# Attention's four units together ahead of the graph convolution, with one denominator fold, in batches 2 to 14

## The chip, the cores and the metric

The kernel runs on one core of one Trainium2 chip. The core has a matrix engine (TensorE, in the profile PE, with its weight loads as PEld), a vector engine (VectorE, DVE), a scalar engine (ScalarE, ACT), a small general engine (GpSimd, POOL) and a synchronisation engine whose queue issues the transfers (SyncE, SP). They run side by side, each strictly in the order of its own instructions, and wait for each other through semaphores. TensorE writes only to PSUM; the other compute engines read it there.

The metric is the device time of one execution in microseconds (us). The kernel before took 2126.58 us, the median of three runs (2126.36 to 2126.92). Lower is better.

## The reference

Sixteen graphs ("batches") of 1024 nodes with 256 channels go through two layers. Cut to what matters:

```python
# layer 0: attention whose queries come from a data-dependent weighting of the adjacency
c_adj = mean(x, channels)                            # one number a node
A  = abs(abs(sigmoid(c_adj[None] - c_adj[:, None]) - .5) - .5) * 2
g  = relu((x.T @ (adj * (A + A.T) / 2)) * para)      # queries, 4 heads of 64
k, v = split(x @ kv_w)
x  = layernorm(x + softmax(q @ k.T * scale) @ v)
# layer 1: two graph convolutions
h  = relu(x @ w1_loop + adj @ (x @ w1_neigh) + b1)
h  = relu(h @ w2_loop + adj @ (h @ w2_neigh) + b2)
x  = layernorm(x + (x + h) * .5)
```

Everything is float32 and everything stays on one core.

## The kernel before, in words

**Stages of a batch.** In the steady state (batches 2 to 14) the kernel works on four batches at once. In the turn of batch b TensorE does, in this order:

1. scores and outputs of attention units 0 and 1 of batch b (a unit is one pair of heads, `pair`, and one half of the 1024 query nodes, `j`; four units in `UNITS`);
2. one joined convolution (`Joined.run`) that does the first convolution of batch b-1 (`c1`) and the second of batch b-2 (`c2`) together, as seven products in the manner of Strassen: products 1, 2, 6, 7, 5, 4, 3 in this order, then seven smaller products with the second layer's weights (`last_products`);
3. scores and outputs of units 2 and 3 of batch b;
4. the queries of batch b+1 (`FastQueries`, seven products for each of four steps, tiles `g_ps`);
5. keys and values of batch b+1 (`KeysValues`).

The scores (`scores`, L702 in the profile before) make 8 tiles of 128 x 1024 a unit in PSUM; ScalarE takes their exponential into rows `pr`; the outputs (`outputs`, L744) multiply them with the values. The softmax denominators are sums of the `pr` rows: VectorE adds the eight rows of a unit (`collect`, L721 and L723), transposes the sum in 32 x 32 blocks and reduces it (`partial`, L728 and L731), and a small product with a constant `fold` on TensorE (`add`, L764) finishes them. `add` then scales the outputs, adds the residual and reduces (L770 to L777). `turn` (L755) takes an output out of PSUM by a block transpose.

**Memories.** Nearly all working data lie in 31 rows of 128 x 1024 in SBUF (tag `row`), given out in turn: a new tile waits for the last readers and writers of the tile that had its place. PSUM is given out in the same way: three tiles of two banks (`big_psum`, `half_psum` takes half of one) and two tiles of one bank (`bank_psum`). Of each four score tiles one is split in two halves over the two single banks (`split` in `scores`: tiles 2 and 6 of unit 0 and 2, and so on); an output takes a half of a big tile (first unit of a pair) or a single bank (second unit).

**What sets the order.** The order on every engine is the order in which the program is written (`manual_schedule`). Nothing is moved by a scheduler; the kernel places VectorE's and ScalarE's work for the queries, the layer norms and the convolution by hand, as functions that run between two products (`between`, called by `turn_to`). SyncE's one queue issues all transfers in program order, and its wait for a row holds back every later transfer. The adjacency is read from memory in each batch, 512 KB a row: seven pairs of rows for the convolution (`Joined.fetch`, L198) and eight rows for the queries (`Queries.load`, L544).

In the turn of batch b the other engines have, beside the above: the likenesses of the queries (`likeness`, two ScalarE passes over 128 x 1024 each, L560 and L561), their product with the adjacency (`times_adj`, L566) and sums (`right`, L619 to L622) on VectorE; sums over 128 x 512 blocks on GpSimd (`Joined.left`, tiles `R`, and `FastQueries.left`, tiles `S`); sums for keys and values on VectorE (`KeysValues.sums`, L423 to L431); two layer norms (`BlockedNorm`; `statistics`, `deviation`, `finish_aside`).

Of the kernel before, what the change touches and what calls it, by code (L numbers as in the profile page):

```python
# [18 lines left out]
def kernel(  # L19
# [310 lines left out]
    def by_node(t):  # L330
        return t.rearrange("p (bn r) -> p bn r", r=S)
# [252 lines left out]
    class FastQueries(Queries):  # L584
# [16 lines left out]
        def block(self, i, j):  # L601
            return self.xb[:, j * TJ:(j + 1) * TJ, ts(i, P)]

        def left(self, eng):
            s12, s34 = (row_tile(f"S_{self.b}_{k}").rearrange("p (s t c) -> p s t c", s=2, c=P) for k in range(2))
            eng.tensor_add(s12[:, 0], self.block(1, 0), self.block(1, 1))
            eng.tensor_sub(s12[:, 1], s12[:, 0], self.block(0, 0))
            eng.tensor_sub(s34[:, 0], self.block(0, 0), self.block(1, 0))
            eng.tensor_sub(s34[:, 1], self.block(0, 1), s12[:, 1])
            self.S = [s12[:, 0], s12[:, 1], s34[:, 0], s34[:, 1]]  # L610
# [63 lines left out]
    class Attention:  # L674
# [5 lines left out]

        def __init__(self, b, xB, qT, kT, v):
            self.b, self.xB, self.qT, self.kT, self.v = b, xB, qT, kT, v
            self.parts, self.o, self.pr = {}, {}, {}

            self.rden = small.tile([P, len(UNITS) * FB // S], F32, tag="rden", name=f"rden_{b}", bufs=2)
            self.sums = small.tile([P, NC, NB], F32, tag="sums", name=f"sums_{b}", bufs=2)
# [38 lines left out]
        def partial(self, u):  # L725
            b = self.b
            accB = row_tile(f"accB_{b}_{u}")
            nc.vector.transpose(accB, self.acc)  # L728
            if u % 2 == 0:
                self.part = small.tile([P, 2, N // S], F32, tag="den_part", name=f"den_part_{b}_{u}", bufs=2)  # L730
            nc.vector.tensor_reduce(self.part[:, u % 2, :], by_node(accB), AX.X, ALU.add)  # L731
            self.parts[u] = self.part

        def both_scores(self, pair, summed=True):
            for j in range(NJ):
# [15 lines left out]
        def turn(self, u):  # L751
# [2 lines left out]
            self.o[u] = work.tile([P, FB], F32, tag="o", name=name) if late else row_tile(name)[:, 0:FB]  # L754
            nc.vector.transpose(self.o[u], pav)  # L755

        def add(self, *units):

            b, half = self.b, FB // S
            u0, n = units[0], len(units)  # L760
            pd = bank_psum(f"den_ps_{b}_{u0}")
            den = pd[:, 0:2 * half * n]
            part = [self.parts.pop(u) for u in units][0]
            nc.tensor.matmul(den, fold.rearrange("p a k -> p (a k)"),  # L764
                             part[:, u0 % 2:u0 % 2 + n, :].rearrange("p u k -> p (u k)"), start=True, stop=True)
            den = den.rearrange("p (u s h) -> p u s h", u=n, s=2)
            rden = self.rden[:, u0 * half:(u0 + n) * half].rearrange("p (u h) -> p u h", u=n)
            for s in range(2):
                rows = slice(s * HD, (s + 1) * HD)
                nc.vector.reciprocal(rden[rows], den[rows, :, s, :])  # L770
            for k, u in enumerate(units):
                pair, j = UNITS[u]
                o = by_node(self.o.pop(u))
                nc.vector.tensor_mul(o, o, rden[:, k, :].unsqueeze(2).to_broadcast([P, half, S]))
                dst = by_node(self.xB[pair][:, ts(j, FB)])
                nc.vector.tensor_add(dst, dst, o)
                nc.vector.tensor_reduce(self.sums[:, pair, ts(j, half)], dst, AX.X, ALU.add)  # L777
            if u == len(UNITS) - 1:
                join(self.sums)
# [324 lines left out]
    class Joined:  # L1104
# [33 lines left out]
        def run(self, between=None, last=None):  # L1138
# [17 lines left out]
            self.product(2, third)  # L1156
            nc.vector.tensor_add(p1, p1, third)
            turn_to(2)
            if last:
                bias(third, b2_sb[:, ts(0, P)])  # L1160
                if c2.w2 is None:
                    c2.load_sums()
            self.product(6, first, again=True)
            nc.scalar.copy(u1, first)
            c1.relu(0, p1)
            turn_to(6)
            self.product(7, second, start=True)
            nc.scalar.copy(p7, second)
            turn_to(7)
            self.product(5, first, again=True)  # L1170
            nc.scalar.copy(u3, first)
# [26 lines left out]
    def run():  # L1198
# [58 lines left out]
        for b in range(B):  # L1257
# [18 lines left out]
                q.times_adj(TJ)  # L1276
                q.right(0)

            def two_units(pair, before_first=lambda: None, before_second=lambda: None):
                u = NJ * pair  # L1280
                att.outputs(u, half_psum, turned=False)
                before_first()
                att.turn(u)
                att.outputs(u + 1, turned=False)
                before_second()
                att.turn(u + 1)

            if more and not c1:
                att.both_scores(0)
                NodeSums(q, xb, str(b + 1)).all()  # L1290
                two_units(0)
                att.both_scores(1)
                for t in range(3):
                    q.load(t)
                    q.weigh(t)
                two_units(1)
            elif more and not both:
                att.scores(0)
                att.outputs(0)
                NodeSums(q, xb, str(b + 1)).all()  # L1300
                kv = KeysValues(b + 1, channel_major(blocked, f"xT_{b + 1}"))
                att.scores(1)
                kv.sums()
                att.add(0)
                att.outputs(1)
                for t in (0, TJ):
                    q.load(t)
                c1.inner()
                q.left(nc.gpsimd)
                for t in (0, TJ):  # L1310
                    q.likeness(t)
                for ij, n in QUARTERS.items():
                    store(n, quarters[ij])
                c1.first(quarters, lambda: (att.add(1), adj_sums(quarters, 1), adj_sums(quarters, 2), weigh_first()))
                c1.turn_blocks()
                att.scores(2)
                att.outputs(2)
                for t in (1, TJ + 1):
                    q.load(t)
                    q.likeness(t)  # L1320
                    q.times_adj(t)
                att.scores(3)
                for t in (2, TJ + 2, 3, TJ + 3):
                    q.load(t)
                for t in (2, TJ + 2, 3, TJ + 3):
                    q.likeness(t)
                q.right(1)
                att.add(2)
                att.outputs(3)
            elif more:  # L1330
                att.both_scores(0, summed=False)
                nodes = NodeSums(q, xb, str(b + 1))
                att.collect(1, 1, 2, 3)
                nodes.turn()
                att.collect(1, *range(4, NT))
                att.partial(1)
                both.fetch("00", "10")
                c2.load_x()

                def next_xT():  # L1340
                    ready["xT"] = channel_major(blocked, f"xT_{b + 1}")

                two_units(0, before_second=next_xT)
                if c3:
                    c3.statistics()
                kv = KeysValues(b + 1, ready["xT"])
                kv.sums()
                both.fetch(2, 3)
                nodes.line()
                both.fetch(1)  # L1350
                nodes.row()
                for t in (0, TJ):
                    q.load(t)
                both.fetch(4, "11")
                c1.inner()
                both.left(nc.gpsimd)
                q.left(nc.gpsimd)
                both.run({1: (lambda: q.likeness(0),),
                          2: (lambda: att.add(0, 1), lambda: q.likeness(TJ), lambda: c3 and c3.deviation(), weigh_first)},
                         last=nc.gpsimd)  # L1360
                c1.turn_blocks()
                att.both_scores(1)
                order = (1, TJ + 1, 2, TJ + 2, 3, TJ + 3)
                for t in order:
                    q.load(t)
                for t in order:
                    q.likeness(t)

                def weigh_second():
                    q.times_adj(1)  # L1370
                    q.times_adj(TJ + 1)
                    q.right(1)

                two_units(1, before_second=weigh_second)
            else:
                att.both_scores(0)
                two_units(0)
                att.both_scores(1)
                two_units(1, before_second=lambda: att.add(0, 1))
# [38 lines left out]
            elif more:  # L1418
                q.pair(2)
                q.step(0)  # L1420
                if c3:
                    c3.finish_aside(out[b - 3])
                q.step(1, lambda: att.add(*((2, 3) if both else (3,))), 5)
                q.pair(3)
                q.step(2, norm.mean)
                q.load_para()
                kv.load()
                q.step(3)
# [107 lines left out]
```

## Time and profile before

The profiled execution took 2127.08 us, 0.50 us above the median of the three runs; its span from first to last instruction is 2125.2 us. The granted TensorE clock was 0.999 of full speed. Stages of the turn of batch 8 (start 1045.54 us, length 130.74 us, as in nearly all turns of batches 3 to 14), from the profile's table by stretches of time:

| stage of the turn | us | DVE busy | ACT busy | POOL busy | GB/s |
|---|---|---|---|---|---|
| scores and outputs, units 0 and 1 | 27.82 | 26.27 | 18.18 | 3.49 | 278 |
| joined convolution | 37.85 | 33.59 | 11.72 | 15.41 | 125 |
| scores and outputs, units 2 and 3 | 27.82 | 25.82 | 20.55 | 0.00 | 128 |
| queries of the next batch | 24.59 | 23.99 | 14.02 | 0.00 | 124 |
| keys and values of the next batch | 12.66 | 10.43 | 7.50 | 4.96 | 172 |
| sum | 130.74 | 120.11 | 71.97 | 23.86 | |

TensorE is busy through all of it. How to read this: "busy" is the time in which an engine executes; a table row of a timeline names the start, the length, the engine, the line of the kernel, the tiles and how many equal instructions follow each other, and in brackets the idle time before and what ended it. A float32 product appears as two matrix instructions, and products with 64 rows of two heads run side by side, so 64 instructions of the scores are 16 tiles.

### The profile page before, as it was taken

How to read it: one execution, taken by the hardware profiler on the slowest of the kernel's cores; microseconds unless marked ns; L12 is line 12 of the kernel's file. 1: busy time of each engine (PE TensorE's matmuls, PEld its weight loads, DVE VectorE, ACT ScalarE, POOL GpSimd, SP SyncE). 2: the span in 40 equal slices, each digit the busy share in tenths (PEclk: the TensorE clock that was granted, in tenths of full speed). 3: DMA queues.
4: the chain of work that ended last, by engine and by line, in shares of the span. 5: the costliest groups of instructions: out<-in, count | busy, mean ns of one | idle time of the engine just before them, and what ended most of it. 6: DMA issues, size and time to landing. Idle time of an engine off the chain costs nothing.

```text
span 2125.2 us, 25170 instructions
## 1 busy us (share of the span) xinstructions
PE 2115.0 (100%) x8734; PEld 1036.0 (49%) x8734; DVE 1907.4 (90%) x2381; ACT 1139.7 (54%) x1669; POOL 358.6 (17%) x209
## 2 busy tenths in 40 slices
PE   9999999999999999999999999999999999999998
PEld 5344444545445455454554444544445444454354
DVE  6899998989999899998989989899898998989975
ACT  5745545555365563655636556355564556555523
POOL 2010120121302213031130311303013130121021
PEclk9999999999999999999999999999999999999999
DMA  9495766637539275492845929468293682934555
GB/s 214 121 179 188 135 228 140 177 107 152 210 109 258 95 146 197 129 273 70 166 170 136 264 70 191 152 152 241 70 221 122 159 233 70 253 100 123 152 167 177
DMA packets 613718, 346.39 MB, mean 163 GB/s; under 512 B 491984, under 2 KB 556880, under 8 KB 613584
## 3 DMA queue, kind: packets, MB, share of 16 engines
q1 hardware_dynamic: 613312, 344.45, 62.0%
q8 instruction: 71, 1.16, 0.2%
q14 instruction: 63, 0.52, 0.1%
q10 hardware_dynamic: 272, 0.26, 0.0%
HBM read 294.45 MB, written 50.20 MB: 162 GB/s over the span
## 4 chain that ended last, share of the span: by engine, by line
PE 97%; SPq 1%; DMA 1%; DVE 0%; ACT 0%; issue 0%; POOL 0%; POOLq 0%; DVEq 0%
PE s L702 21%; PE av L744 21%; PE hu_ps L1135 17%; PE g_ps L647 16%; PE v_ps L448 4%; PE k_ps L444 4%; PE hu_ps L972 4%; PE t_ps L858 3%; PE hu_ps L865 2%; PE g_ps L574 1%; PE h_ps L880 1%; PE u_ps L909 1%; PE h_ps L972 1%; SPq L108 1%; SPq L229 0%; DMA adj<-in_adj_dram 0%
## 5 line engine op out<-in xcount | busy, mean ns | idle before, releaser
L723 DVE TENSOR_TENSOR acc<-acc,pr 128x1024 f32<-128x1024 f32 x384 | 472.2, 1230 | 37.4 <-DVE acc L723 1.4
L702 PE MATMUL s<-qT,kT 64*128 64x512 f32 x2048 | 449.7, 593 | 0.2 <-ACT qT L581 0.2
L744 PE MATMUL av<-pr,v 128*64 128x512 f32 x2048 | 447.0, 594 | 0.0
L709 ACT ACTIVATE pr<-s 128x1024 f32<-128x1024 f32 x392 | 391.8, 1122 | 75.3 <-PE s L702 75.2
L702 PEld LDWEIGHTS s<-qT,kT 64*128 64x128 f32 x2048 | 196.3, 187 | 233.0 <-issue 183.0
L744 PEld LDWEIGHTS av<-pr,v 128*64 128x64 f32 x2048 | 144.0, 137 | 297.4 <-issue 272.9
L361 POOL TENSOR_TENSOR rstd<-rstd,neg_half 128x32 f32<-128x32 f32 x16 | 99.2, 6203 | 1112.8 <-DVE rstd L359 1112.8
L1135 PE MATMUL hu_ps<-adj,R 128*128 128x512 f32 x480 | 214.3, 594 | 0.0
L560 ACT ACTIVATE wg<-c_row,c_sums 128x1024 f32<-128x1024 f32 x120 | 137.0, 1142 | 81.4 <-DVE den_part L731 60.3
L566 DVE SCALAR_TENSOR_TENSOR wg<-wg,adj 128x1024 f32<-128x1024 f32 x128 | 150.0, 1210 | 3.6 <-ACT wg L561 3.6
L707 ACT ACTIVATE pr<-s 128x512 f32<-128x512 f32 x240 | 143.3, 710 | 0.3 <-PE s L702 0.3
L1135 PEld LDWEIGHTS hu_ps<-adj,R 128*128 128x128 f32 x480 | 89.0, 190 | 100.9 <-issue 98.8
L561 ACT ACTIVATE wg<-wg 128x1024 f32<-128x1024 f32 x128 | 135.3, 1057 | 4.1
L861 ACT COPY t<-t_ps 128x1024 f32<-128x1024 f32 x16 | 16.2, 1012 | 189.8 <-PE t_ps L858 189.8
L647 PE MATMUL g_ps<-wg,S 128*128 128x512 f32 x224 | 115.6, 597 | 0.0
L647 PE MATMUL g_ps<-T,S 128*128 128x512 f32 x224 | 115.5, 597 | 0.0
L647 PE MATMUL g_ps<-wg,x 128*128 128x512 f32 x224 | 109.0, 599 | 0.0
L1135 PE MATMUL hu_ps<-adj,t 128*128 128x512 f32 x240 | 105.7, 592 | 0.0
L1126 POOL TENSOR_TENSOR R<-h 128x512 f32<-128x512 f32 x14 | 28.2, 2012 | 359.5 <-PE av L744 238.5
L721 DVE TENSOR_TENSOR acc<-pr,pr 128x1024 f32<-128x1024 f32 x64 | 77.5, 1210 | 11.9 <-ACT pr L709 11.9
L728 DVE STREAM_TRANSPOSE accB<-acc 128x1024 f32<-128x1024 f32 x64 | 79.7, 1245 | 2.2
L731 DVE TENSOR_REDUCE den_part<-accB 128x32 f32<-128x1024 f32 x64 | 78.1, 1220 | 2.2
(235 smaller groups left out, 3116.9 us busy)
## 6 DMA issues: line engine op xcount, KB each, us to landing
adj<-adjT SPq DMA_DIRECT2D x210, 512.0 KB
adj<-in_adj_dram SPq DMA_DIRECT2D x128, 512.0 KB
para<-in_L_gnn_para_dram SPq DMA_DIRECT2D x32, 512.0 KB
xB_a<-in_x_dram SPq DMA_DIRECT2D x128, 128.0 KB
x1d<-xB_a SPq DMA_DIRECT2D x128, 128.0 KB
x<-x1d SPq DMA_DIRECT2D x16, 1024.0 KB
xB<-in_x_dram SPq DMA_DIRECT2D x120, 128.0 KB
x<-in_x_dram SPq DMA_DIRECT2D x15, 1024.0 KB
```

Of the source, the lines that this page charges most:

```text
L361: nc.gpsimd.tensor_tensor(self.rstd, self.rstd, neg_half, ALU.pow)
L560: nc.scalar.activation(wg, self.c_row, AF.Abs, bias=self.c_col[:, t:t + 1], scale=-1.0)
L561: nc.scalar.activation(wg, wg, AF.Tanh, scale=-0.5 / C)
L566: nc.vector.scalar_tensor_tensor(wg, wg, 1.0, self.adj.pop(t), op0=ALU.add, op1=ALU.mult)
L647: nc.tensor.matmul(self.p[n], x_n[:, k, :], w_n, start=(k == 0), stop=(k == TJ - 1))
L702: nc.tensor.matmul(halves[s], self.kT[rows, pair, ts(mt, P)], self.qT[rows, pair, ts(j, FB)], start=True, stop=True)
L707: nc.scalar.activation(pr[:, ts(s, FB)], halves[s], AF.Exp)
L709: nc.scalar.activation(pr, ps, AF.Exp)
L723: nc.vector.tensor_add(self.acc, self.acc, prs[mt])
L744: nc.tensor.matmul(pav[s * HD:(s + 1) * HD, :], self.v[:, mt, pair * P + s * HD:pair * P + (s + 1) * HD], prs[mt][:, ts(s, FB)], start=(mt ...
L972: nc.tensor.matmul(dst[:, ts(t, P)], a[:, ts(t, P)], w, start=first, stop=True, skip_group_check=not first)
L1135: nc.tensor.matmul(dst, self.x[n][:, k, :], of_rows(rows, k), start=(start and k == 0), stop=(k == TJ - 1), skip_group_check=again)
```

## The change

In batches 2 to 14 (the branch with both convolutions) the order of the turn becomes: units 0 and 1, units 2 and 3, joined convolution, queries, keys and values. What moves with it:

- `both_units` replaces `both_scores` and `two_units` there. The first unit of a pair adds up its rows as its scores come; of the second unit the additions follow on VectorE, with the block transpose of the first output between the fifth and the sixth addition, and that of the second output after `partial`. Both outputs go into the halves of one row. NodeSums and its transpose (`sums`, `nodes.turn`), the two first query rows' likenesses and the first transfers for the convolution stand between them.
- `add_all` replaces the two calls of `add`: one fold over the denominators of all four units (a 128 x 128 product in place of two of 128 x 64), two reciprocals in place of four, and multiplication, addition and reduction on 1024 columns at a time (six instructions in place of twelve). It stands after product 2 of the convolution. `den_part` becomes one tile for all units.
- The query rows are weighed in another order: 0 and 4 during attention and after product 1, 1 and 5 between products 1 and 4, 2, 6, 3 and 7 after the convolution's last products, with the layer norm's `finish_aside` behind them.
- VectorE's transpose of the next batch's input (`channel_major`) comes after all of attention; GpSimd's query sums `S` go into the rows of that input (`q.left(nc.gpsimd, blocked)`); the layer norm's statistics and deviation follow together; the sums for keys and values move to the last step of the queries.
- In `Joined.run` ScalarE's copy of the bias into the third bank comes after product 7's copy, not after product 2.
- The transfers: convolution rows 00 and 10 and query rows 0 and 4 are fetched during units 2 and 3, then 2 and 3; 1, query rows 1 and 5, 4 and 11 after them. The store of the first layer's output (`turn_blocks`) comes after the whole convolution and now stands right ahead of the queries.

```diff
+        def both_units(self, pair, first=lambda: None, second=lambda: None, third=lambda: None):
+            u = NJ * pair
+            self.scores(u, 0)
+            self.scores(u + 1, NT, summed=False)
+            row = row_tile(f"o_{self.b}_{pair}")
+            self.collect(u + 1, 1)
+            first()
+            self.collect(u + 1, 2, 3)
+            second()
+            self.outputs(u, half_psum, turned=False)
+            self.collect(u + 1, 4, 5)
+            pav, self.o[u] = self.o[u], row
+            nc.vector.transpose(row[:, 0:FB], pav)
+            self.collect(u + 1, 6, 7)
+            self.partial(u + 1)
+            self.outputs(u + 1, turned=False)
+            third()
+            nc.vector.transpose(row[:, FB:N], self.o.pop(u + 1))
+
+        def add_all(self):
+            b, half, n = self.b, FB // S, len(UNITS)
+            pd = bank_psum(f"den_ps_{b}")
+            nc.tensor.matmul(pd[:, 0:n * NB], fold.rearrange("p a k -> p (a k)"),
+                             self.part.rearrange("p u k -> p (u k)"), start=True, stop=True)
...
+            for pair in range(NC):
+                o = by_node(self.o.pop(NJ * pair))
+                nc.vector.tensor_mul(o, o, self.rden[:, ts(pair, NB)].unsqueeze(2).to_broadcast([P, NB, S]))
+                dst = by_node(self.xB[pair])
+                nc.vector.tensor_add(dst, dst, o)
+                nc.vector.tensor_reduce(self.sums[:, pair, :], dst, AX.X, ALU.add)
+            join(self.sums)
...
             turn_to(2)
-            if last:
-                bias(third, b2_sb[:, ts(0, P)])
-                if c2.w2 is None:
-                    c2.load_sums()
+            if last and c2.w2 is None:
+                c2.load_sums()
             self.product(6, first, again=True)
...
             nc.scalar.copy(p7, second)
+            if last:
+                bias(third, b2_sb[:, ts(0, P)])
             turn_to(7)
...
             elif more:
-                att.both_scores(0, summed=False)
-                nodes = NodeSums(q, xb, str(b + 1))
-                att.collect(1, 1, 2, 3)
-                nodes.turn()
-                att.collect(1, *range(4, NT))
-                att.partial(1)
-                both.fetch("00", "10")
-                c2.load_x()
...
-                two_units(0, before_second=next_xT)
...
+                att.both_units(0, sums, lambda: nodes.turn())
+                nodes.line()
+                nodes.row()
+                att.both_units(1, before_convolution, third=lambda: (q.times_adj(0), q.times_adj(TJ)))
+                c1.inner()
+                xT_next = channel_major(blocked, f"xT_{b + 1}")
+                both.left(nc.gpsimd)
+                q.left(nc.gpsimd, blocked)
...
-                both.run({1: (lambda: q.likeness(0),),
-                          2: (lambda: att.add(0, 1), lambda: q.likeness(TJ), lambda: c3 and c3.deviation(), weigh_first)},
+                both.run({1: (lambda: q.likeness(1), lambda: q.likeness(TJ + 1), lambda: q.right(0)),
+                          2: (att.add_all,),
+                          4: (lambda: q.times_adj(1), lambda: q.times_adj(TJ + 1)),
+                          3: (more_weights, lambda: q.right(1))},
                          last=nc.gpsimd)
                 c1.turn_blocks()
-                att.both_scores(1)
...
-                two_units(1, before_second=weigh_second)
...
                 q.pair(2)
                 q.step(0)
-                if c3:
-                    c3.finish_aside(out[b - 3])
-                q.step(1, lambda: att.add(*((2, 3) if both else (3,))), 5)
+                if both:
+                    q.step(1)
+                else:
+                    q.step(1, lambda: att.add(3), 5)
                 q.pair(3)
                 q.step(2, norm.mean)
+                if both:
+                    kv.sums()
```

More of the change, by code (lines that the diff above doesn't have):

```diff
@@ L602, in block, with left @@
             return self.xb[:, j * TJ:(j + 1) * TJ, ts(i, P)]
-        def left(self, eng):
-            s12, s34 = (row_tile(f"S_{self.b}_{k}").rearrange("p (s t c) -> p s t c", s=2, c=P) for k in range(2))
+        def left(self, eng, rows=None):
+            rows = rows or [row_tile(f"S_{self.b}_{k}") for k in range(2)]
+            s12, s34 = (row.rearrange("p (s t c) -> p s t c", s=2, c=P) for row in rows)
             eng.tensor_add(s12[:, 0], self.block(1, 0), self.block(1, 1))
@@ L682, in __init__ @@
             self.b, self.xB, self.qT, self.kT, self.v = b, xB, qT, kT, v
-            self.parts, self.o, self.pr = {}, {}, {}
+            self.o, self.pr = {}, {}
             self.rden = small.tile([P, len(UNITS) * FB // S], F32, tag="rden", name=f"rden_{b}", bufs=2)
@@ L728, in partial @@
             nc.vector.transpose(accB, self.acc)
[L729 to L732, printed above, removed]
+            if u == 0:
+                self.part = small.tile([P, len(UNITS), N // S], F32, tag="den_part", name=f"den_part_{b}", bufs=1)
+            nc.vector.tensor_reduce(self.part[:, u, :], by_node(accB), AX.X, ALU.add)
         def both_scores(self, pair, summed=True):
@@ L755, in turn @@
             nc.vector.transpose(self.o[u], pav)
+        def both_units(self, pair, first=lambda: None, second=lambda: None, third=lambda: None):
[21 more added lines that the diff above has]
+                             self.part.rearrange("p u k -> p (u k)"), start=True, stop=True)
+            den = pd[:, 0:n * NB].rearrange("p (u s h) -> p u s h", u=n, s=2)
+            rden = self.rden.rearrange("p (u h) -> p u h", u=n)
+            for s in range(2):
+                rows = slice(s * HD, (s + 1) * HD)
+                nc.vector.reciprocal(rden[rows], den[rows, :, s, :])
+            for pair in range(NC):
[5 more added lines that the diff above has]
+            join(self.sums)
         def add(self, *units):
@@ L762, in add @@
             den = pd[:, 0:2 * half * n]
-            part = [self.parts.pop(u) for u in units][0]
             nc.tensor.matmul(den, fold.rearrange("p a k -> p (a k)"),
-                             part[:, u0 % 2:u0 % 2 + n, :].rearrange("p u k -> p (u k)"), start=True, stop=True)
+                             self.part[:, u0:u0 + n, :].rearrange("p u k -> p (u k)"), start=True, stop=True)
             den = den.rearrange("p (u s h) -> p u s h", u=n, s=2)
@@ L1277, in weigh_first, with two_units @@
                 q.right(0)
-            def two_units(pair, before_first=lambda: None, before_second=lambda: None):
+            def two_units(pair, before_second=lambda: None):
                 u = NJ * pair
                 att.outputs(u, half_psum, turned=False)
-                before_first()
                 att.turn(u)
@@ L1330, in run @@
             elif more:
-                att.both_scores(0, summed=False)
-                nodes = NodeSums(q, xb, str(b + 1))
-                att.collect(1, 1, 2, 3)
-                nodes.turn()
-                att.collect(1, *range(4, NT))
-                att.partial(1)
-                both.fetch("00", "10")
-                c2.load_x()
-                def next_xT():
-                    ready["xT"] = channel_major(blocked, f"xT_{b + 1}")
-                two_units(0, before_second=next_xT)
@@ L1344, in run, with sums, before_convolution @@
-                if c3:
[L1345 to L1349, printed above, removed]
+                nodes = None
+                def sums():
+                    nonlocal nodes
+                    nodes = NodeSums(q, xb, str(b + 1))
+                    c2.load_x()
+                def before_convolution():
+                    both.fetch("00", "10")
+                    for t in (0, TJ):
+                        q.load(t)
+                        q.likeness(t)
+                    both.fetch(2, 3)
@@ new lines, in run @@
+                att.both_units(0, sums, lambda: nodes.turn())
[6 more added lines that the diff above has]
+                q.left(nc.gpsimd, blocked)
+                if c3:
+                    c3.moments()
+                kv = KeysValues(b + 1, xT_next)
@@ L1350, in run, with more_weights @@
                 both.fetch(1)
-                nodes.row()
-                for t in (0, TJ):
+                for t in (1, TJ + 1):
                     q.load(t)
                 both.fetch(4, "11")
-                c1.inner()
-                both.left(nc.gpsimd)
-                q.left(nc.gpsimd)
-                both.run({1: (lambda: q.likeness(0),),
-                          2: (lambda: att.add(0, 1), lambda: q.likeness(TJ), lambda: c3 and c3.deviation(), weigh_first)},
+                def more_weights():
+                    for t in (2, TJ + 2, 3, TJ + 3):
+                        q.load(t)
+                        q.likeness(t)
+                    if c3:
+                        c3.finish_aside(out[b - 3])
@@ L1360, in run @@
+                both.run({1: (lambda: q.likeness(1), lambda: q.likeness(TJ + 1), lambda: q.right(0)),
+                          2: (att.add_all,),
+                          4: (lambda: q.times_adj(1), lambda: q.times_adj(TJ + 1)),
+                          3: (more_weights, lambda: q.right(1))},
                          last=nc.gpsimd)
                 c1.turn_blocks()
-                att.both_scores(1)
-                order = (1, TJ + 1, 2, TJ + 2, 3, TJ + 3)
-                for t in order:
-                    q.load(t)
@@ L1366, in run @@
[L1366 to L1372, printed above, removed]
-                two_units(1, before_second=weigh_second)
             else:
```

## The prediction

> **What bounds the kernel now.** I read the page first: engine shares, then the chain that ended last.
>
> ```profile
> span 2125.2 us, 25170 instructions
> PE 2115.0 (100%) x8734; PEld 1036.0 (49%) x8734; DVE 1907.4 (90%) x2381; ACT 1139.7 (54%) x1669; POOL 358.6 (17%) x209
> PE 97%; SPq 1%; DMA 1%; DVE 0%; ACT 0%; issue 0%; POOL 0%; POOLq 0%; DVEq 0%
> ```
>
> The chain is TensorE almost alone, so only two things can change the time: TensorE's own instructions, and a wait put in front of one. TensorE's timeline of the turn of batch 8 shows how little slack there is (start, length, tiles, count):
>
> ```profile
> 1045.54 14.00 PE L702 MATMUL s<-qT,kT 64*128 64x512 f32 x64
> 1059.47 13.95 PE L744 MATMUL av<-pr,v 128*64 128x512 f32 x64
> 1073.36 3.84 PE L858 MATMUL t_ps<-w1n_sb,x1T 128*128 128x128 f32 x32
> ...
> 1103.01 1.05 PE L972 MATMUL hu_ps<-w2n_sb,uT 128*128 128x128 f32 x8
> 1103.90 1.06 PE L972 MATMUL h_ps<-w2l_sb,h1T 128*128 128x128 f32 x8
> ...
> 1110.23 1.06 PE L972 MATMUL hu_ps<-w2l_sb,last 128*128 128x128 f32 x8
> 1111.21 14.00 PE L702 MATMUL s<-qT,kT 64*128 64x512 f32 x64
> ...
> 1139.03 1.98 PE L647 MATMUL g_ps<-wg,x 128*128 128x512 f32 x4
> 1140.85 1.02 PE L647 MATMUL g_ps<-wg,S 128*128 128x512 f32 x2
> ...
> 1147.72 0.33 PE L764 MATMUL den_ps<-den_part,fold 128*128 128x64 f32 x2
> ```
>
> No row has idle time before it; the next turn begins at 1176.28, 130.74 us on. Third, VectorE's timeline of units 0 and 1, because the second output leaves PSUM only at its end:
>
> ```profile
> 1066.93 0.20 DVE L290 STREAM_TRANSPOSE c_turned<-c_sums 128x32 f32<-128x32 f32 x1
> 1067.06 4.99 DVE L723 TENSOR_TENSOR acc<-acc,pr 128x1024 f32<-128x1024 f32 x4
> 1072.08 1.25 DVE L728 STREAM_TRANSPOSE accB<-acc 128x1024 f32<-128x1024 f32 x1
> 1073.36 1.22 DVE L731 TENSOR_REDUCE den_part<-accB 128x32 f32<-128x1024 f32 x1
> 1074.50 0.71 DVE L755 STREAM_TRANSPOSE o<-av 128x512 f32<-128x512 f32 x1
> ```
>
> VectorE lags: TensorE is done with these units at 1073.36, VectorE takes the first output out at 1074.50. Today the convolution follows and needs that bank late. Fourth, the last batch, 15: it has no new queries and already runs its units back to back. Its timelines (TensorE, then all engines):
>
> ```profile
> 1961.10 14.00 PE L702 MATMUL s<-qT,kT 64*128 64x512 f32 x64
> 1988.92 15.06 PE L702 MATMUL s<-qT,kT 64*128 64x512 f32 x64
> 1990.34 1.30 DVE L755 STREAM_TRANSPOSE o<-av 128x512 f32<-128x512 f32 x2
> 1991.70 0.30 PEld L702 LDWEIGHTS s<-qT,kT 64*128 64x128 f32 x4 [0.77 <-DVE o L755]
> ```
>
> The scores of units 2 and 3 take 1.06 us longer there (15.06 against 14.00): a weight load waits for the block transpose that frees the bank. It starts 0.06 us after it.
>
> **What the change takes off TensorE.** One fold of two: the fold at 1147.72 and the two g instructions behind it end at 1148.80, 1.08 us, where two g instructions alone take 0.86, so a fold costs 0.22 us. A fold of 32 columns (sum_ps at 1154.81, next pair ends at 1155.89) costs 0.22 too, so I give the wider fold 0.22; it has twice the columns, and at most 0.11 more (128-column instructions are 0.111 us apart, 0.89 for 8). Saved 0.22, bounds 0.11 and 0.22. Second, changes of tile form: conv to scores costs 0.98-0.89 = 0.09 us (1110.23 to 1111.21 against 1103.01 to 1103.90), and the first four g instructions after outputs take 1.82 us where four later ones take 1.71 (1145.15 to 1146.86), 0.11. After the change outputs lead into scores, which pay what scores paid, and the convolution leads into g, both of 128 x 128 form. Saved 0.20; bounds 0 (every seam costs the same) and 0.40 (outputs to scores free). Together 0.42 us a turn.
>
> **What it puts in.** In the built order of the changed kernel, the second half of score tile 2 of unit 2 takes the single bank of output 1, and waits for its transpose. On VectorE that stands behind: scale and transposes of the norm, unit 0's additions, unit 1's additions with output 0's transpose between the fifth and sixth, accB, den_part. The row above puts the first L755 at 1074.50-1045.54 = 28.96 us after the turn's start. Output 0 moves in front of it. It adds 0.63 (1074.50 to the next instruction, 1075.13), less what it hides of the dependent additions' latency: they stand 1.25 apart, two independent transposes (2.33 for two of 1.20) 1.13 apart, so 0.51 net. Output 1's transpose ends at 28.96+0.51+0.71 = 30.18, that is 2.36 after the scores of unit 2 begin (27.82). In batch 15 the corresponding end is 1991.64-1988.92 = 2.72 after them, and cost 1.06. So here 1.06-(2.72-2.36) = 0.70 us. Bounds: 0.19, were output 0 free, and 0.82, were nothing hidden. I take 0.70: the same wait, 0.36 us earlier. Everything queued behind that weight load on TensorE, all of the turn, is late by it. ScalarE and VectorE wait for those scores anyway (ScalarE is 1.1 us behind TensorE there), and catch nothing up for a full TensorE.
>
> An ordinary turn thus changes by 0.70-0.42 = +0.28 us. Batch 2 is worse: VectorE makes the last adjacency sums before its norm there (scale starts at 264.41, 3.49 after the turn's 260.92, against 1.42), so 2.07 more.
>
> **What I cost at nothing, with its cover.** Times from the turn's start; convolution products then start at 61 us, g at 94, keys at 118.
> - VectorE: den_part of unit 3 ends near 55, two times_adj (1.21 each), output 3, the input's transposes (2.33) and the statistics (4.3) bring it to 65, where product 1 has freed the rows `right` writes. `right` runs beside GpSimd's S. At 1097.36 a sum beside GpSimd took 1.64, the next 1.75, alone 0.69; so four cost 2.8 to 7.0. Then 0.7 for the product-2 addition, 0.7 for reciprocals, 7.3 for `add_all` (six of 1.22): 76 to 81. The next need is product 4 at 82, and its own user is at 86: 1 to 6 us, then 4 more. Beyond it each us would cost a us. The K sums move away from S: four of 1.65 to 1.76 become 0.69. In the queries `right(3)` ends near 109, ahead of step 3 at 112; in the kernel before it ended at 1158.87, 113 after its turn's start (VectorE, 1158.18 and 0.69).
> - ScalarE: four likenesses and finish_aside (8.6 + 4.0 us) after 93 end at 106; next need is g's first copy at 114. The bias copy (0.59) near 77, need 86.
> - GpSimd: R 1.27 each, done by 65 (need 69 to 84); S by 71 (need 94); norm power 2.6 behind S, by 74; uT lower needs it free at 80.
> - SP: convolution rows wait for attention rows to be read, 25 to 57 us; the last eight of 0.5 MB go out at 52 to 57 and take 11 us at the 377 to 408 GB/s that such rows reach. Needs 75 to 84. Query row 4 waits for unit 2's den_part (43) and holds the queue; need 55. w2 sums out at 69, need 87.
> - The store of h1 (4 transfers of 128 KB, 128 B packets, took 4 us from 1114) now stands between out and para, kv_sums. Those moved from 1154 to 1162, that is until 116.5; now 116.5-1.6 (finish_aside earlier)+4 = 119, need of kv_sums 121.6. Cover 2.6 us.
>
> The Trainium skill, "SBUF — State Buffer", Who interferes with whom, speaks against the `right` beside S: a VectorE instruction with two SBUF inputs and a GpSimd read exclude each other, the loser waiting out the whole instruction. By it `right` could lose all of S, an estimate of 6.3 us, and end still inside the cover above; the rows (1 us an instruction) give at most 4.2.
>
> The same skill, "TensorE: Matmul & The Clock Gate", warns of gaps over about 3 us, after which the clock halves; batch 15's wait left the granted clock at 0.999 over the run, and no row here shows a 3 us gap.
>
> **Sum**, against the profiled execution (2127.08, 0.50 above the median): 13 turns of +0.28 = 3.6, batch 2's 2.07 more, 5.7; 2132.8 profiled, 2132.3 as median. A measurement here tells 0.2%, 4.25 us, from no change: 5.7 is just over.
>
> **Rivals.**
> 1. The wait is there and shorter. GpSimd's power before the norm takes 6.35 us in most turns, 5.44 at 1171.32; there VectorE was 0.46 earlier. Everywhere, that makes the turn -0.18: 2.1-2.4 = -0.3, time 2126. For: one row. Against: all others.
> 2. (faster) The wait disappears. It costs nothing if the transpose ends 0.70 earlier, 1.66 after the scores begin; also if TensorE's running ahead with the other head made up for it. Then only the saving is left, 13 x 0.42 = 5.5, less 1.4 still lost in batch 2: 2122.5, or 2121.1 with none. Against: batch 15 ran ahead too and lost 1.06.
> 3. A second wait. kv_sums after its need, or VectorE late at product 4. Each us beyond the cover (2.6, and 1 plus 4) costs 13 us: 2135 to 2150. For: transfers wait on eight earlier ones in turn, which I cannot time. Against: every cover above is over 2 us but one.
>
> **Chances.** Forecast 0.60, 2129 to 2135; over 2130.8 in 0.50 of it, as the saving's bounds (0.11 to 0.62) move it by -2.6 to +4. Rival 1 0.14, rival 2 0.09, rival 3 0.17. Slower 0.50+0.17 = 0.67, same 0.10+0.14 = 0.24, faster 0.09. Range 2125 to 2140: it leaves out rival 2 and a third of rival 3.
>
> **What will show it.** TensorE: L703 of units 2 and 3 near 14.6 where 14.0, released by DVE o L774, 16 to 17 in batch 2; then no idle up to the next turn; turn 131.0; one 128-column fold of 0.22; g's first four in 1.71. Wrong if that run takes 13.9, if TensorE idles at k_ps behind a transfer or at hu_ps behind VectorE.

## The result, and the profile after

The changed kernel takes **2132.63 us**, the median of nine runs (2131.72 to 2133.94), against 2126.92 for the kernel before on the same chip: a ratio of 1.0028, 95% interval 1.0017 to 1.0038. It is 0.3% slower. The forecast was 2132.3.

The page of the changed kernel (its first lines, and the chain that ended last) looks almost like the one before. TensorE is busy for 99% of the span, where it was 100%; in the chain it has one point less (96% for 97%), VectorE and ScalarE one more each:

```profile
span 2132.2 us, 24959 instructions
...
PE 2119.8 (99%) x8708; PEld 1083.0 (51%) x8708; DVE 1874.6 (88%) x2277; ACT 1134.1 (53%) x1669; POOL 348.1 (16%) x209
...
PE 96%; DVE 1%; SPq 1%; DMA 1%; ACT 1%; issue 0%; POOL 0%; POOLq 0%; DVEq 0%; ACTq 0%
```

VectorE does 33 us less and the kernel is slower. The waits of the weight loads, over the whole execution, name what is new (`s` are the scores, `o` the outputs; the columns are the sum, the number of times and the longest, in us):

```profile
PEld s L703 <- DVE o L774: 7.2, 13, 2.4
```

Thirteen times, once a turn, a weight load of the scores waits for the block transpose at the end of `both_units`. The turn of batch 8, TensorE's timeline (start, length, tiles, count):

```profile
1050.50 14.00 PE L703 MATMUL s<-qT,kT 64*128 64x512 f32 x64
1064.43 13.95 PE L744 MATMUL av<-pr,v 128*64 128x512 f32 x64
1078.32 14.66 PE L703 MATMUL s<-qT,kT 64*128 64x512 f32 x64
1092.91 13.95 PE L744 MATMUL av<-pr,v 128*64 128x512 f32 x64
1106.80 3.84 PE L894 MATMUL t_ps<-w1n_sb,x1T 128*128 128x128 f32 x32
...
1119.06 0.38 PE L779 MATMUL den_ps<-den_part,fold 128*128 128x128 f32 x2
1119.28 10.46 PE L1171 MATMUL hu_ps<-adj,R 128*128 128x512 f32 x24
1129.58 3.60 PE L1171 MATMUL hu_ps<-adj,h 128*128 128x512 f32 x8
...
1143.66 1.06 PE L1008 MATMUL hu_ps<-w2l_sb,last 128*128 128x128 f32 x8
1144.55 1.88 PE L648 MATMUL g_ps<-wg,x 128*128 128x512 f32 x4
1146.27 1.02 PE L648 MATMUL g_ps<-wg,xB 128*128 128x512 f32 x2
...
1181.47 0.70 PE L703 MATMUL s<-qT,kT 64*128 64x512 f32 x2
```

The turn is 1181.47-1050.50 = 130.97 us long, 0.23 more than the 130.74 before. From start to start, the scores of units 2 and 3 take 1092.91-1078.32 = 14.59 where those of units 0 and 1 take 13.93: 0.66 us lost. Everything else got shorter, by 0.43 in all. There is one fold, and no second one among the g products. From its start to the end of the 24 products behind it is 1129.58-1119.06 = 10.52 us, the same as in the kernel before, where the fold has half the columns (1085.62 to 1096.14). The convolution's last products lead into g in 0.89 and not 0.98, and the first four g instructions take 1.72 and not 1.82.

VectorE's timeline and one row of the weight loads show what the 0.66 waits for:

```profile
1074.41 0.71 DVE L769 STREAM_TRANSPOSE o<-av 128x512 f32<-128x512 f32 x1
1075.05 2.44 DVE L724 TENSOR_TENSOR acc<-acc,pr 128x1024 f32<-128x1024 f32 x2
1077.52 1.25 DVE L729 STREAM_TRANSPOSE accB<-acc 128x1024 f32<-128x1024 f32 x1
1078.80 1.22 DVE L732 TENSOR_REDUCE den_part<-accB 128x32 f32<-128x1024 f32 x1
1079.94 0.71 DVE L774 STREAM_TRANSPOSE o<-av 128x512 f32<-128x512 f32 x1
```

```profile
1080.70 3.30 PEld L703 LDWEIGHTS s<-qT,kT 64*128 64x128 f32 x17 [0.37 <-DVE o L774]
```

TensorE was done with output 1 at 1078.4. VectorE adds, transposes and reduces until 1079.9 before it takes it out of its bank; the transpose ends at 1080.65 and the weight load starts at 1080.70. The bracket says only 0.37, because some instructions of the other head run ahead first. What the wait costs is the 0.66 by which the run of scores is longer.

Batch 2 is a case of its own. In this profiled execution its units 2 and 3 take 18.35 for the scores, 4.42 more than 13.93:

```profile
292.38 0.71 DVE L774 STREAM_TRANSPOSE o<-av 128x512 f32<-128x512 f32 x1
...
293.14 0.30 PEld L703 LDWEIGHTS s<-qT,kT 64*128 64x128 f32 x4 [2.43 <-DVE o L774]
293.14 5.40 PE L703 MATMUL s<-qT,kT 64*128 64x512 f32 x16 [1.60 <-DVE o L774]
```

The wait accounts for 2.72 of it (the runs below show that length alone). The rest is the clock: behind the wait, eight instructions took 0.97 to 1.05 us each in place of 0.59. The table by stretches has the stretch from 293 to 297, with the granted clock in the third column from the right:

```profile
293.00:297.00 4.00, 3.86 (x10) 1.67 (x12) 2.42 (x3) 1.08 (x2) 0.00 (x0) 0.58 0.82 296
```

So this execution, 2133.94, lies 1.3 above the median. Summed over turns without that fall (batch 2's turn is then 133.03, 2.29 longer than 130.74): 12 x 0.22 + 2.29 = 4.9 us, of the 5.7 between the medians. Most of the rest stands behind the last turn. From the first scores of the last batch to the end it is 164.1 us in the kernel before, and 164.5, 164.8 and 165.0 in three profiles of the changed kernel; in all three, 0.36 of it lies ahead of the last small product (`good_ps`). What causes it was not tested. Other parts vary from one execution to the next: a few turns of 130.93 in the kernel before, one of 131.3 after, and the beginning, where the first scores start anywhere between 48.2 and 49.9 us.

### The profile page after: what moved, and what is told of

Read it like the earlier page. It is cut to its first block, busy times and chain, and to the rows that moved or that the text cites. A ratio compares the mean times of both kernels' runs of the same rounds, so it can differ in the third digit from the quotient of the medians.

```text
span 2132.2 us, 24959 instructions
## 1 busy us (share of the span) xinstructions
PE 2119.8 (99%) x8708; PEld 1083.0 (51%) x8708; DVE 1874.6 (88%) x2277; ACT 1134.1 (53%) x1669; POOL 348.1 (16%) x209
## 4 chain that ended last, share of the span: by engine, by line
PE 96%; DVE 1%; SPq 1%; DMA 1%; ACT 1%; issue 0%; POOL 0%; POOLq 0%; DVEq 0%; ACTq 0%
PE s L703 21%; PE av L744 20%; PE hu_ps L1171 17%; PE g_ps L648 16%; PE v_ps L448 4%; PE k_ps L444 4%; PE hu_ps L1008 4%; PE t_ps L894 3%; PE hu_ps L901 2%; PE g_ps L574 1%; PE h_ps L916 1%; PE u_ps L945 1%; PE h_ps L1008 1%; DVE acc L724 1%; SPq L108 1%; SPq L229 0%
## 5 line engine op out<-in xcount | busy, mean ns | idle before, releaser
L724 DVE TENSOR_TENSOR acc<-acc,pr 128x1024 f32<-128x1024 f32 x384 | 481.6, 1254 | 37.3 <-ACT pr L708 2.1
L703 PE MATMUL s<-qT,kT 64*128 64x512 f32 x2048 | 460.8, 596 | 1.9 <-DVE o L774 1.6
L703 PEld LDWEIGHTS s<-qT,kT 64*128 64x128 f32 x2048 | 247.0, 187 | 204.1 <-issue 135.2
L648 PE MATMUL g_ps<-wg,xB 128*128 128x512 f32 x208 | 107.3, 597 | 0.0
L648 PE MATMUL g_ps<-T,xB 128*128 128x512 f32 x208 | 106.2, 592 | 0.0
```

The costliest lines, as they stand in the source:

```text
L648: nc.tensor.matmul(self.p[n], x_n[:, k, :], w_n, start=(k == 0), stop=(k == TJ - 1))
L703: nc.tensor.matmul(halves[s], self.kT[rows, pair, ts(mt, P)], self.qT[rows, pair, ts(j, FB)], start=True, stop=True)
L724: nc.vector.tensor_add(self.acc, self.acc, prs[mt])
```

## The experiments

Theory A is the prediction's: the late transpose is the whole loss. Its rivals are a further wait behind it; VectorE's lateness as such, whatever the bank; and covers that are gone (a cover is the time by which an engine may be late before TensorE waits for it). Times are medians; ratios are to the kernel before.

**The transpose ahead of `partial`** (units 0 and 1 alone):

```diff
-            self.partial(u + 1)
             self.outputs(u + 1, turned=False)
+            if pair == 0:
+                nc.vector.transpose(row[:, FB:N], self.o.pop(u + 1))
+            self.partial(u + 1)
             third()
-            nc.vector.transpose(row[:, FB:N], self.o.pop(u + 1))
+            if pair == 1:
+                nc.vector.transpose(row[:, FB:N], self.o.pop(u + 1))
```

> Only the place of one VectorE instruction changes: in units 0 and 1 the block transpose that frees the single bank of output 1 stands ahead of `partial`, no longer behind it. It should end about 28.7 us after the turn's start (when output 1 is ready, 27.9, and 0.7 more), 0.9 after the scores of unit 2 begin. Theory A (this wait is all that the change costs): the scores of unit 2 take 13.93 again, the turn 130.96-0.66 = 130.30, batch 2 keeps 0 to 0.4 of its 4.42, and the time is 2132.6 - 12 x 0.66 - 4.2 = 2120.5 us, faster than both kernels by 0.3%. Theory B (another wait stands right behind, a row or a score tile of VectorE's later work): 2126 to 2133, with TensorE idle at another tile in the same stretch.

Measured: 2122.94 us, ratio 0.998 (0.9971 to 0.9989). Ordinary turns are 130.31, and in them the loss is gone to the last hundredth. TensorE's timeline, then VectorE's, in the turn of batch 8:

```profile
1043.69 14.00 PE L703 MATMUL s<-qT,kT 64*128 64x512 f32 x64
1057.63 13.95 PE L744 MATMUL av<-pr,v 128*64 128x512 f32 x64
1071.51 14.00 PE L703 MATMUL s<-qT,kT 64*128 64x512 f32 x64
```

```profile
1071.63 0.72 DVE L773 STREAM_TRANSPOSE o<-av 128x512 f32<-128x512 f32 x1 [0.95 <-PE av L744]
1072.27 1.20 DVE L729 STREAM_TRANSPOSE accB<-acc 128x1024 f32<-128x1024 f32 x1
```

VectorE now idles 0.95 us until TensorE has the output, and that idle time costs nothing. The transpose ends 0.84 after the scores of unit 2 begin. The time is 2.4 us above the expectation. It took away batch 2's 4.2, which had the fall of the clock in it; a usual execution has only 2.72 to lose there, and 0.19 of it stays (14.12 for the scores, a turn of 130.50). With that, 2132.6 - 12 x 0.65 - (133.03-130.50) = 2122.3. What makes up the 0.6 that is left stays open.

**Another bank**, VectorE's order as in the changed kernel:

```diff
-            self.outputs(u + 1, turned=False)
+            self.outputs(u + 1, bank_psum if pair else half_psum, turned=False)
```

> The changed kernel with VectorE's order kept, but output 1 in half of a big PSUM tile, no longer in a single bank. The second half of score tile 2 then has a bank that is long free; the transpose, still ending 2.3 us (batch 2: 4.4) after the scores of unit 2 begin, is waited for by score tile 3, which comes at 3 x 1.74 = 5.2 us. Theory A: the scores of unit 2 take 13.93 in all turns, batch 2 too, the turn is 130.30, and the time is that of the early transpose less 0 to 0.3: about 2122.7 us. If it is VectorE's lateness itself that holds TensorE, through whatever tile: as the changed kernel, 2132.6. If two outputs in the three big tiles leave the scores too few of them: above 2132.6, with TensorE idle at score tiles 0 to 3.

Measured: 2123.57, ratio 0.9984 (0.9975 to 0.9993). Ordinary turns are 130.31 again, although the transpose is as late as in the changed kernel. So VectorE's lateness in itself holds nothing; which score tile gets output 1's bank decides. The expectation for batch 2 was wrong. It took 1.74 us for one score tile. But 16 tiles in 13.93 are 0.87 each, so tile 3 comes at 2.6 us, before the transpose's end at 4.4, and batch 2 loses 15.80-13.93 = 1.87 there:

```profile
292.59 0.30 PEld L703 LDWEIGHTS s<-qT,kT 64*128 64x128 f32 x4 [2.42 <-DVE o L774]
```

**The wait made longer.** A reduction is repeated right ahead of the late transpose, over half or the whole of its data (the whole is shown):

```diff
             nc.vector.tensor_reduce(self.part[:, u, :], by_node(accB), AX.X, ALU.add)
+            self.accB = accB
...
             self.partial(u + 1)
+            if pair == 0:
+                nc.vector.tensor_reduce(self.part[:, u + 1, :], by_node(self.accB), AX.X, ALU.add)
             self.outputs(u + 1, turned=False)
```

> One reduction of 128 x 512 (about 0.6 us) is repeated on VectorE right ahead of the transpose that frees output 1's bank, in units 0 and 1. Theory A (the wait passes on every microsecond): the scores of unit 2 take 14.59 + 0.6 = 15.2, the turn 131.6, the time 2132.6 + 13 x 0.6 = 2140.4 us. Theory C (in batch 2 of the changed kernel the granted clock fell to 0.58 for 4 us after a stall of this kind, and a stall near 1.3 us already brings that on): about 1.8 us more in each turn, 2163. Theory D (VectorE has slack there and the wait is not VectorE's lateness): no change, 2132.6.

> As the one before with a whole reduction of 128 x 1024 (1.14 us) repeated: the delay ahead of the transpose is doubled. Theory A: the scores of unit 2 take 14.59 + 1.14 = 15.73, the turn 132.1, the time 2132.6 + 13 x 1.14 = 2147.5 us. Theory C (the granted clock falls after such a stall, as in batch 2): 1.8 us more a turn in all or some turns, up to 2171. Theory D: no change. The Trainium skill (TensorE: Matmul & The Clock Gate, Why this matters for your kernels) has the clock fall after gaps of over about 3 us; by it neither this run nor the last would see it fall.

Measured: 2141.81 (ratio 1.007, 1.0054 to 1.0085) and 2150.61 (1.0112, 1.0097 to 1.0128). The rows of VectorE in the second, with the whole reduction, batch 8:

```profile
1084.21 1.22 DVE L732 TENSOR_REDUCE den_part<-accB 128x32 f32<-128x1024 f32 x1
1085.46 1.22 DVE L774 TENSOR_REDUCE den_part<-accB 128x32 f32<-128x1024 f32 x1
1086.60 0.70 DVE L777 STREAM_TRANSPOSE o<-av 128x512 f32<-128x512 f32 x1
```

From the first reduction's start to the transpose's start it is 2.39 and was 1.14, so the repeat costs 1.25 and not 1.14 (0.72 for the half). The scores of units 2 and 3 take 15.84 with the whole and 15.30 with the half, that is 1.25 and 0.71 more than 14.59. The wait passes on VectorE's delay to the hundredth. In ordinary turns of the two profiled executions the clock stays up, behind gaps of up to 1.73 us between the starts of two TensorE instructions. With the whole reduction the profiled execution took 2147.69, and the three others took 2.0 to 3.9 us more. Their mean granted clock is 0.998, 0.997 and 0.997, against 0.999: 0.1 to 0.2% of 2150 us is 2.2 to 4.3 us, an estimate, so the clock may account for it; no profile shows in which turns.

In batch 2, where the wait is longest, the clock fell with the half, behind a gap of 2.91 us (first row, the third column from the right), and not with the whole, behind one of 3.43 (second row):

```profile
294.00:298.00 4.00, 4.00 (x14) 1.62 (x12) 2.65 (x3) 2.33 (x3) 0.00 (x0) 0.57 0.60 241
```

```profile
293.50:297.50 4.00, 3.79 (x18) 1.85 (x20) 3.16 (x4) 2.37 (x3) 0.00 (x0) 1.00 0.82 269
```

**The control on the kernel before**, with the same reduction repeated ahead of its own second output's transpose:

```diff
...
+            def again():
+                nc.vector.tensor_reduce(att.part[:, 1, :], by_node(att.accB), AX.X, ALU.add)
...
-                two_units(0, before_second=next_xT)
+                two_units(0, before_second=lambda: (again(), next_xT()))
```

> The control, on the kernel before: there too a reduction of 128 x 1024 (1.14 us) is repeated right ahead of the transpose that takes output 1 out of its bank, in batches 2 to 14. Theory A (VectorE is as late there, but after units 0 and 1 comes the convolution, which needs that bank late): no change, 2127.0 us, turn 130.74. If VectorE's lateness costs whatever comes next, because it is busy through the convolution as well: up to 13 x 1.14 = 14.8 us more, 2141.8.

Measured: 2127.32, ratio 1.0001 (0.9992 to 1.001). Turns stay at 130.74. VectorE's rows and TensorE's, in the turn that starts at 1046.26:

```profile
1075.86 1.18 DVE L1281 TENSOR_REDUCE den_part<-accB 128x32 f32<-128x1024 f32 x1
1076.96 2.36 DVE L238 STREAM_TRANSPOSE xT<-xB 128x1024 f32<-128x1024 f32 x2
1079.24 0.67 DVE L756 STREAM_TRANSPOSE o<-av 128x512 f32<-128x512 f32 x1
```

```profile
1060.20 13.95 PE L745 MATMUL av<-pr,v 128*64 128x512 f32 x64
1074.08 3.84 PE L859 MATMUL t_ps<-w1n_sb,x1T 128*128 128x128 f32 x32
1077.76 1.88 PE L866 MATMUL hu_ps<-x1T,w1l_sb 128*128 128x512 f32 x4
```

The transpose ends 5.8 us after TensorE left the units, later than in any turn of the changed kernel, and TensorE goes on. With the convolution behind the outputs, nothing on TensorE wants that bank so early.

**Two folds in place of one** in `add_all`:

```diff
-            nc.tensor.matmul(pd[:, 0:n * NB], fold.rearrange("p a k -> p (a k)"),
-                             self.part.rearrange("p u k -> p (u k)"), start=True, stop=True)
+            for k in range(0, n, NJ):
+                nc.tensor.matmul(pd[:, k * NB:(k + NJ) * NB], fold.rearrange("p a k -> p (a k)"),
+                                 self.part[:, k:k + NJ, :].rearrange("p u k -> p (u k)"), start=True, stop=True)
```

> The one fold product of 128 columns in `add_all` is made as two of 64 columns again, everything else as in the changed kernel. If a fold costs TensorE 0.22 us whatever its width: 13 x 0.22 = 2.9 us more, 2135.5 us. If its cost goes with the columns, or its issue hides beside the products: 0 to 0.5 us more, 2132.6 to 2133.1, and the saving of 0.44 us a turn is all from the order of the stages.

Measured: 2136.12, ratio 1.0042 (1.0029 to 1.0056). Turns are 131.19, 0.23 longer than 130.96. The two folds (four instructions) and the products behind them, batch 8:

```profile
1119.61 0.55 PE L780 MATMUL den_ps<-den_part,fold 128*128 128x64 f32 x4
1120.00 10.52 PE L1172 MATMUL hu_ps<-adj,R 128*128 128x512 f32 x24
1130.36 3.60 PE L1172 MATMUL hu_ps<-adj,h 128*128 128x512 f32 x8
```

That is 1130.36-1119.61 = 10.75, 0.23 more than the 10.52 with one fold of 128 columns or one of 64. So half of the 0.44 saved in a turn is the fold, and its width does not matter; the other half is left to the changes of tile form. In this kernel the wait of batch 2 left the clock alone: its scores of units 2 and 3 took 16.65.

**The cover of `add_all`.** Each of its two reductions is made twice, or three times:

```diff
-                nc.vector.tensor_reduce(self.sums[:, pair, :], dst, AX.X, ALU.add)
+                for _ in range(2):
+                    nc.vector.tensor_reduce(self.sums[:, pair, :], dst, AX.X, ALU.add)
```

> As the run with three reductions, with two each: VectorE is 2.3 us later behind product 2, up to 3.2 if one of the additions behind it falls beside a GpSimd sum as it did there (2.17 in place of 1.23). The cover of 4.0 us (1.51 of idle time, 2.5 until TensorE reads uT) holds both: no change, 2132.6 us, turn 130.96. Were VectorE's lateness there handed on: 2132.6 + 13 x 2.3 = 2162.

> The cover of `add_all`: its two reductions (1.14 us each) are made three times each, so that VectorE is 4.6 us later behind product 2. In the changed kernel's profile VectorE then idles 1.51 us at 1131.76 and hands over uT at 1133.96, which TensorE needs at 1136.45: 4.0 us of cover. If that is the nearest need: 0.6 us a turn, 2132.6 + 13 x 0.6 = 2140 us. If the cover is 5 us or more, as the prediction had it at most: 2132.6. If there is none and VectorE's lateness is handed on whole: 2132.6 + 13 x 4.6 = 2192.

Measured: twice, 2132.55, turns 130.96, as the changed kernel. Three times, 2160.1 (ratio 1.0154, 1.0138 to 1.0169): turns of 133.07 to 133.56, 2.1 more and not 0.6. Rows of the second, from VectorE's, GpSimd's and TensorE's timelines in the turn that starts at 1061.77:

```profile
1142.79 2.17 DVE L790 TENSOR_TENSOR xB_a<-xB_a,o 128x1024 f32<-128x1024 f32 x1
...
1148.76 0.19 DVE L275 TENSOR_TENSOR sums<-sums 128x32 f32<-128x32 f32 x1
```

```profile
1141.71 2.17 POOL L1213 TENSOR_TENSOR uT<-snap 128x512 f32<-128x512 f32 x1 [6.50 <-ACT snap L1208]
1143.95 2.13 POOL L996 TENSOR_TENSOR last<-h1T,uT 128x512 f32<-128x512 f32 x1
```

```profile
1149.72 1.16 PE L1009 MATMUL hu_ps<-w2n_sb,uT 128*128 128x128 f32 x8 [1.84 <-DVE uT L1212]
```

The cover of 4.0 us was read rightly; the work put in is more than the 4.6 reckoned. The four repeats start 1.25 apart and not 1.14, 5.0 in all, and one addition on VectorE, 1.23 in the changed kernel, now runs beside a GpSimd sum and takes 2.17, as the GpSimd sum does (1.27 before). VectorE's `join` behind the sums (L275) starts 87.0 us after the turn's start, against 81.0 in the changed kernel: 6.0 later. Of these the cover takes 4.0, and 6.0-4.0 = 2.0 is left, of the 2.1 that the turn is longer.

**Batch 15 as well.** Its second unit's `partial` is put behind both transposes, beside the early transpose of the first run:

```diff
-                att.both_scores(0)
+                att.both_scores(0, summed=False)
+                att.collect(1, *range(1, NT))
                 two_units(0)
+                att.partial(1)
```

> The early transpose, and the same order in batch 15: its second unit's `partial` behind both transposes of the outputs. There the scores of units 2 and 3 take 14.99 in both kernels. Theory A: they take 13.93 with it, 1.06 us less than the early transpose alone (2122.9): 2121.9. If batch 15 waits for something else: 2122.9.

Measured: **2121.5 us**, ratio 0.9975 (0.9964 to 0.9985), the fastest of all, 0.4 below the expectation. The last batch's scores of units 2 and 3 take 13.93:

```profile
1968.71 13.95 PE L744 MATMUL av<-pr,v 128*64 128x512 f32 x64
1982.59 14.00 PE L703 MATMUL s<-qT,kT 64*128 64x512 f32 x64
1996.52 1.94 PE L744 MATMUL av<-pr,v 128*64 128x512 f32 x8
```

**The changed kernel again, twice**, for the clock in batch 2:

> The changed kernel itself once more, for batch 2 alone. In its first profile the granted clock fell to 0.58 behind a 2.19 us gap (start to start) between two score products, and units 2 and 3 took 18.35; with two folds in place of one the same gap of 2.19 left the clock at full and they took 16.65. If the fall comes with the stall: 18.35 again. If it depends on when in an execution the stall falls: 16.65 in some executions, and then 1.7 us less in all.

> The same as the one before it: 18.35 if the stall decides, 16.65 or 18.35 if its moment does.

Measured: 2132.26 and 2132.64, with 16.65 for batch 2's scores in both, behind the same gap of 2.19. The stretch that had a clock of 0.58, in the first of them:

```profile
293.00:297.00 4.00, 3.98 (x20) 1.86 (x21) 3.16 (x3) 2.56 (x4) 0.00 (x0) 1.00 0.92 304
```

The same wait may or may not pull the clock down.

## Why the prediction was right, point by point

- **The new wait.** The transpose was put at 30.18 us after the turn's start; it ends at 1080.65-1050.50 = 30.15. Its price was 0.70, taken from batch 15's wait as "the same wait, 0.36 us earlier"; it is 0.66. That it is this wait and no other is shown from two sides: with the transpose early, and with another bank, the scores take 13.93.
- **The saving.** 0.42 was forecast, 0.22 for the fold and 0.20 for the changes of form; the turn shows 130.74+0.66-130.97 = 0.43. The fold's half was undone and came back as 0.23. The other half was read from rows (0.89 for 0.98, 1.72 for 1.82) and not undone by itself.
- **The net of an ordinary turn**: +0.28 forecast, +0.22 to 0.23 measured, the two small errors adding up.
- **The total** is right in part by luck. Of the 5.7 us forecast the turns give 4.9; the median comes within 0.3 us of the forecast with the help of the program's end, which the prediction did not reckon with and which takes 0.4 to 0.9 us more in the three profiles.
- **Batch 2.** Forecast 0.70+2.07 = 2.77, measured 2.72 where the clock held. What the prediction missed there was the clock. The prediction let it rest at full speed because "batch 15's wait left the granted clock at 0.999" and no row showed a gap of 3 us; in one of three profiles of the changed kernel it fell for 4 us behind a gap of 2.19, for 1.7 us more. The Trainium skill ("TensorE: Matmul & The Clock Gate", Why this matters for your kernels) warns of gaps over about 3 us; here the measurement decides, and 2.19 between two starts was enough once.
- **The covers.** `right(0)` beside S took 0.68, 1.65, 1.76 and 1.58, 5.7 in all, within the 2.8 to 7.0 given (in the turn of batch 8); `add_all` ended at 81.3, just behind the range of 76 to 81; two more reductions, 2.5 us, cost nothing there. No weight load of the keys or of the convolution waits for a transfer.
- **Rival 1** (a shorter wait, with a power of 5.44 us on GpSimd) did not occur: it took 6.35 or 6.36 ahead of all thirteen turns. **Rival 2** (no wait) is what the early transpose makes of the kernel: 2122.9, against 2122.5 worked out for it. That they agree so closely is luck in part: the sum has 1.4 us still lost in batch 2, with no working given, and the run lost 0.19 there. **Rival 3** (a second wait) is not there, but its price is right: past a cover of 4 us, each us costs 13 (2.1 a turn came to 27.5 us).

## What to carry to other kernels

When stages change places, ask of each PSUM bank who takes it next and how soon; the engine that empties it may come 5.8 us late with one successor at no cost, and set the time at 2.3 us with another. The cure is then to empty the bank before work nobody waits for, or to give the next user a bank that is free: either turned the 0.3% lost into 0.2% gained here. A cover read from idle time plus slack held to a tenth of a us, but work pushed to its end can fall beside another engine's and grow.

## What the runs showed of the hardware that was not expected

- The granted clock fell behind a gap of 2.19 us between two of TensorE's starts (to 0.58 over 4 us, in one of three profiled executions of the same program) and behind one of 2.91 (0.57, with the half reduction repeated). It did not fall behind one of 3.43 (the whole reduction), nor behind those of 2.35 to 2.44 that each of the thirteen turns has with the sums made three times. The length of the gap alone does not decide; when it falls may, but that was not tested.
- A reduction repeated on the same output starts 1.25 us after the first, where different work starts 1.14 after it.
- TensorE's running ahead with the other head gains nothing against a longer delay: it shortens the idle time in the bracket, and the delay added still reaches the end of the run of scores whole (1.25 of 1.25).
